# Two Fourier-attention layers on image planes: a kernel whose planes are normalized, mixed and squared in place, against one that keeps everything linear in modes and in one Gram matrix

## Chip, core and metric

The kernel runs on one core of one Trainium2 chip. The core has a matrix engine (TensorE, in the profile PE, with its weight loads as PEld), a vector engine (VectorE, DVE), a scalar engine (ScalarE, ACT), a general engine (GpSimd, POOL) and queues that start DMA transfers (SP, and the ACT queue). The metric is the device time of one execution in microseconds (us): 1426.25 us before the change, the median of three runs (1425.6 to 1430.25). A profiled execution is a run of its own; its span goes from its first instruction to its last.

## The reference

The input x holds 2 batches of 56 images of 128 x 128, all float32. Two layers of the same form follow each other; each adds its result to x. A layer first takes a group norm over the batch's images (32 groups of 4 neighbouring columns), and then:

```
xn   = inorm(xa)                          # each image: mean 0, variance 1
k, q, v = Spec(xn) + skip(xn)             # 1 -> 8 heads
attn = softmax(<q, k> / 128)              # 56 x 56 per head and batch
out  = Spec(attn v) + skip(attn v)        # 8 heads -> 1
att  = inorm(out + xa);  an = inorm(att)
h    = gelu(inorm(Spec(an)) + skip(an))   # M0
h    = inorm(Spec(h)) + skip(h)           # M1
y    = inorm(h) + att
```

`Spec` is a spectral convolution: the two-dimensional real Fourier transform, 32 x 16 of its modes multiplied by weights, and the transform back. `skip` multiplies by a number per head.

## The kernel before

Two sets of planes stay on chip, `X` (the running x) and `A` (work), each with h on the 128 partitions and (image, w) along them: 112 images of 128 columns. The modes of all images are tiles `spec` of 128 partitions (32 j + 16 c + kx, with c the real or imaginary part) by 8 t by 112 images. `layer` runs for each of the two layers, and does in this order:

- Group norm, per batch: sums over h by a matrix of ones (L340), subtraction (L350), squares (L352) and their sums (L353), scaling (L364), statistics of every image (L326), instance norm (L376, L378).
- Planes to modes: `to_rows` (L270, 112 matmuls of 64 columns with an image as weights), `to_modes` (L282, on four column tiles of 32; L289 exchanges real and imaginary part).
- `U xh` for eight heads (L386 to L388) while TensorE takes the Gram matrices (L394, 128 matmuls per batch, operands read at one w of all images). Scores (L406), softmax, the attention transposed.
- `D`, the output's modes: transposes (L446), products (L453) and sums over heads (L454, L455).
- The mix of images, in place, four w at a time: transposes (L462), copy (L464), matmuls (L467), copy back.
- `from_modes` three times (output, M0, M1): the modes go out to memory and come back turned (L300, L303), POOL reorders them (L308), matmuls on two column tiles (L312), a copy (L316), and matmuls of 512 columns (L319) into a use of its own: L474, L542 with gelu (L545), L557. Between them `to_rows` and `to_modes` again for M0 and M1, their norms (L508 to L528) and the residual (L538).
- The end: instance norm of h and the sum into `X` (L578 to L582); the second layer stores it.

`prepare` (L163) multiplies the weights of a layer out on POOL. A planner puts the instructions of each engine into an order by readiness and by their place in the source; buffers come from pools (`pm` four PSUM banks, `t2` four tiles, `spec` six). Every call of a float32 matmul becomes two weight loads and two matmul instructions; a transpose becomes one of each.

## Time and profile before

| what | value |
|---|---|
| median of three runs | 1426.25 us |
| span of the profiled execution | 1412.7 us |
| clock granted to TensorE, mean over the span | 0.747 |
| HBM read, written | 11.93 MB, 10.09 MB |
| DVE busy | 819.8 us |
| ACT busy | 306.0 us |
| POOL busy | 211.9 us |

The profile gives for each engine the time in which it ran an instruction. The clock line (PEclk) gives the speed that TensorE was granted, in tenths of full speed; 0.50 in a window is half speed. A row of the groups reads: line, engine, operation, output tile and input tiles, their shapes (partitions x elements), count, then busy time, mean time of one in ns, and the idle time of the engine ahead of it with what ended it. A row of the timeline reads: start, length, engine, line, operation, count. Matmul records overlap, so the length of a run divided by its count is the time from one to the next.

### The profile page before, as it was taken

What the parts mean: (1) busy time and instruction counts of PE and PEld (TensorE: products, weight loads), DVE (VectorE), ACT (ScalarE), POOL (GpSimd) and SP (SyncE); (2) the same over time, 40 slices, a digit from 0 to 9 for tenths busy, and PEclk for the clock granted to TensorE, in tenths of its full rate; (3) what the DMA queues carried; (4) which work ended last, traced back from release to release, by engine and by line L of the source; (5) the groups of instructions that cost most, each with busy time, mean ns of one, the idle gap of its engine ahead of it and who ended that gap; (6) DMA issues with size and microseconds to landing.
All of it is one profiled execution on the core that took longest, in us unless ns stands there. A gap on an engine that the chain in (4) does not pass through costs nothing.

```text
span 1412.7 us, 13545 instructions
## 1 busy us (share of the span) xinstructions
PE 1003.7 (71%) x4992; PEld 695.5 (49%) x4992; DVE 819.8 (58%) x2052; ACT 306.0 (22%) x536; POOL 211.9 (15%) x259
## 2 busy tenths in 40 slices
PE   5374899798778936948633849989877887287550
PEld 1151788346664823724212438944566556146320
DVE  2367452791116797528978581739411397873498
ACT  0222200002221203410352321010122112152024
POOL 6603040000001013011131110400000001301102
PEclk9777599665558977979866957986555599599685
DMA  9000000001000010010000000000100000100106
GB/s 260 0 1 1 0 1 1 1 0 26 0 1 1 1 27 0 1 27 1 1 0 1 0 0 1 1 0 0 26 0 1 0 1 0 27 1 1 26 16 193
DMA packets 38872, 22.89 MB, mean 16 GB/s; under 512 B 8606, under 2 KB 37654, under 8 KB 38806
## 3 DMA queue, kind: packets, MB, share of 16 engines
q1 hardware_dynamic: 37216, 20.19, 5.8%
q10 hardware_dynamic: 1590, 1.83, 0.5%
q8 instruction: 39, 0.64, 0.2%
q14 instruction: 27, 0.22, 0.1%
HBM read 11.93 MB, written 10.09 MB: 16 GB/s over the span
## 4 chain that ended last, share of the span: by engine, by line
PE 60%; DVE 22%; ACT 8%; issue 3%; DMA 3%; POOL 3%; SPq 1%; ACTq 0%; POOLq 0%; DVEq 0%
PE mm L270 12%; PE acc L394 9%; PE mm L467 9%; PE mm L319 9%; DVE rows L326 6%; PE mm L453 5%; PE acc L353 3%; PE mm L312 3%; ACT t L464 3%; DVE A L364 2%; DVE A L580 2%; DVE A L557 2%; PE mm L462 2%; PE acc L340 2%; ACT A L128 2%
## 5 line engine op out<-in xcount | busy, mean ns | idle before, releaser
L319 PE MATMUL mm<-c_gw,t 128*128 128x512 f32 x336 | 168.8, 646 | 31.1 <-ACT t L316 31.1
L270 PEld LDWEIGHTS mm<-c_fh,A 128*128 128x128 f32 x1344 | 168.7, 206 | 8.5 <-issue 3.9
L270 PE MATMUL mm<-c_fh,A 128*128 128x64 f32 x1344 | 172.8, 291 | 0.0
L467 PE MATMUL mm<-mixT,t 112*128 112x112 f32 x512 | 131.2, 438 | 46.5 <-ACT t L464 46.5
L467 PEld LDWEIGHTS mm<-mixT,t 112*128 112x128 f32 x512 | 114.1, 328 | 72.8 <-ACT t L464 72.8
L308 POOL COPY lc<-spec 64x128 f32<-64x128 f32 x84 | 52.7, 655 | 627.7 <-PE mm L312 339.0
L126 DVE COPY A<-mm 128x448 f32<-128x448 f32 x32 | 29.1, 908 | 188.2 <-PE mm L467 188.2
L326 DVE BATCH_NORM_STATS2 rows<-A 128x6 f32<-128x128 f32 x672 | 137.0, 275 | 0.1
L394 PE MATMUL acc<-A 128*56 128x56 f32 x1024 | 134.0, 312 | 0.0
L394 PEld LDWEIGHTS acc<-A 128*56 128x56 f32 x1024 | 128.6, 226 | 6.1 <-issue 3.2
L319 PEld LDWEIGHTS mm<-c_gw,t 128*128 128x128 f32 x336 | 65.2, 205 | 108.1 <-issue 52.9
L126 DVE COPY big<-mm 128x512 f32<-128x512 f32 (+1 forms) x50 | 48.2, 971 | 98.6 <-PE mm L270 98.2
L312 PE MATMUL mm<-c_gh,lc 64*64 64x128 f32 x672 | 51.1, 297 | 75.0 <-POOL lc L308 75.0
L128 ACT COPY big<-mm 128x512 f32<-128x512 f32 (+1 forms) x50 | 47.8, 956 | 204.5 <-PE mm L270 138.9
L312 PEld LDWEIGHTS mm<-c_gh,lc 64*64 64x64 f32 x672 | 40.0, 145 | 104.0 <-POOL lc L308 76.1
L353 PE MATMUL acc<-t,ones_gn 128*128 128x512 f32 x112 | 57.1, 665 | 47.6 <-ACT t L352 47.6
L453 PE MATMUL mm<-attnT,big 56*128 56x448 f32 x128 | 82.8, 822 | 3.7 <-DVE spec L454 3.6
L542 DVE SCALAR_TENSOR_TENSOR A<-A,s,mm 128x128 f32<-128x128 f32 x224 | 59.4, 341 | 28.3 <-PE mm L319 28.3
L316 ACT COPY t<-mm 128x512 f32<-128x512 f32 x42 | 24.6, 586 | 220.6 <-PE mm L312 220.6
L462 PE MATMUL mm<-c_ident,A 128*112 128x128 f32 x256 | 68.0, 421 | 0.0
L340 PE MATMUL acc<-X,ones_gn 128*128 128x512 f32 x112 | 60.4, 688 | 10.1 <-DMA X<-x 7.6
L464 ACT COPY t<-mm 112x512 f32<-112x512 f32 x64 | 37.5, 586 | 136.5 <-PE mm L462 136.5
(170 smaller groups left out, 1239.9 us busy)
## 6 DMA issues: line engine op xcount, KB each, us to landing
X<-x SPq DMA_DIRECT2D x14, 512.0 KB, 7.3
out<-X SPq DMA_DIRECT2D x28, 256.0 KB, 2.3
turned<-spec SPq DMA_DIRECT2D x48, 56.0 KB, 2.0
spec<-turned SPq DMA_DIRECT2D x12, 224.0 KB, 3.7
raw<-weights ACTq DMA_DIRECT2D x2, 544.0 KB, 5.0
c_gw<-const_gw ACTq DMA_DIRECT2D x1, 256.0 KB, 5.3
sm<-small ACTq DMA_DIRECT2D x2, 63.0 KB, 5.5
c_swap<-const_swap ACTq DMA_DIRECT2D x1, 64.0 KB, 5.7
```

Of the source, the lines that this page charges most:

```text
L126: nc.vector.tensor_copy(to, of)
L270: nc.tensor.matmul(py[:, 64 * e : 64 * e + 64], lhsT=A[:, i + e, :], rhs=fh, start=True, stop=True)
L312: nc.tensor.matmul(pz[64 * c : 64 * c + 64, N * e : N * e + N], lhsT=four, rhs=gh[:, c, :], start=True, stop=True,)
L319: nc.tensor.matmul(po, lhsT=z[:, N * e : N * e + N], rhs=gw, start=True, stop=True)
L326: nc.vector.bn_stats(rows[:, k, :], A[:, i, :])
L340: nc.tensor.matmul(acc, lhsT=ones_gn, rhs=X[:, i : i + 4, :], start=(i == lo), stop=(i + 4 == hi))
L353: nc.tensor.matmul(acc2, lhsT=ones_gn, rhs=sq, start=(i == lo), stop=(i + 4 == hi))
L394: nc.tensor.matmul(acc[:K, :K], lhsT=plane, rhs=plane, start=(w == 0), stop=(w == N - 1))
L453: nc.tensor.matmul(pv, lhsT=XT[:, b, n, t, :], rhs=aT[b], start=True, stop=True)
L462: nc.tensor.transpose(pt[:I, N * e : N * e + N], A[:, :, w + e], ident)
L464: nc.scalar.copy(xt[:I, :], pt[:I, :])
L467: nc.tensor.matmul(po[:, I * e : I * e + I], lhsT=xt[:I, N * e : N * e + N], rhs=mix, start=True, stop=True)
```

## The change

The whole of `fno_layers` and the constants are new; the weights' packing and the launch stay.

- **Layouts.** x lies as `X2`, images on 112 partitions (and two rows more, for the group norm's shift), with h and w along them. A second set `P` (`plane`) has w on the partitions, then h, then images. x is loaded in 16 pieces; `turned` transposes 8 rows of h at a time on TensorE, copies them into `plane` on ScalarE, and takes statistics on VectorE.
- **Norms.** The group norm is a factor and a shift per w and batch; it is applied to `plane` in eight chunks inside the first forward transform (`norm`), and to `X2` by `scale_x`. The means and variances of all instance norms come from the Gram matrix of the planes (`gram`, 128 matmuls of 112 x 112) and from sums over modes (`sums`).
- **Transforms.** `forward` contracts w with 32 columns of weights on four column tiles, transposes blocks of 32 x 32 on VectorE, and contracts h; `inverse` goes back to h in the same way and leaves kx on groups of 32 partitions. Nothing goes through memory.
- **Modes.** The multiplication of modes by weights is a matmul with 64 x 64 matrices that POOL builds (`build`, `build_m`). Scores, value products (`VT`), `D`, and the multipliers of M0 and M1 (`multiply`) use them on 64-row tiles. Four PSUM pairs of two banks serve all of it.
- **Planes are met three times**: when they are transposed, in the gelu loop, and in the output loop, where the old x is fetched again from memory (`back`). Layer 0 stores its result in memory, and transposes it for layer 1 at once.
- The scaled planes, with the attention's mix in the weights `Bs`, are multiplied in those two loops in place of the old mix.

The core of the diff:

```diff
-    X = planes.tile([N, I, N], F32, name="X")
-    A = planes.tile([N, I, N], F32, name="A")
+    X2 = xp.tile([J, N, N], F32, name="X2")
+    P = pp.tile([N, N * I], F32, name="P")
...
+    def turned(hs, rows):
+        p = pair()
+        for k, h in enumerate(hs):
+            for e in range(4):
+                T.transpose(p[:, k, I * e : I * e + I], X2[:I, h + e, :], ident[:I, :I])
+        dst = bass_slice(hs[0], hs[1] - hs[0])
+        S.copy(dst, p[:, :, : 4 * I].rearrange("p k (h i) -> p k h i", i=I))
+        for b in range(B):
+            V.bn_stats(rows[b], dst[:, :, :, K * b : K * b + K])
...
+    def forward(xf, prep=None):
+        mid = mp.tile([N, 32, I], F32, name="mid")
+        for c in range(0, 8, 2):
+            p = pair()
+            for k in range(2):
+                i = 14 * (c + k)
+                if prep:
+                    prep(c + k)
+                for q in range(4):
+                    T.matmul(
+                        p[32 * q : 32 * q + 32, k, :448].rearrange("p (h i) -> p h i", h=32),
+                        lhsT=C["fw"], rhs=plane[:, 32 * q : 32 * q + 32, i : i + 14], start=True, stop=True,
+                        tile_position=(0, 32 * q),
+                    )
+            V.transpose(
+                mid[:, :, 14 * c : 14 * c + 28].rearrange("p m (k i) -> p k i m", k=2),
+                p[:, :, :448].rearrange("p k (h i) -> p k i h", h=32),
+            )
...
+        for h in range(N):
+            T.matmul(gram, lhsT=plane[:, h, :], rhs=plane[:, h, :], start=(h == 0), stop=False)
...
+        scale_x(0, 8)
...
+        for t in range(8):
+            p = pair()
+            for r in range(2):
+                for a4 in range(4):
+                    for e in range(2):
+                        k = e ^ r
+                        T.matmul(
+                            p[64 * e : 64 * e + 64, k, I * a4 : I * a4 + I],
+                            lhsT=WU[64 * e : 64 * e + 64, t, 4 * k + a4, :], rhs=xf[64 * e : 64 * e + 64, t, :],
+                            start=True, stop=True, tile_position=(64 * e, 64 * e), skip_group_check=True,
+                        )
+            u = UX[t % 3]
+            evict(u.rearrange("p (k a) i -> p k (a i)", k=2), p[:, :, :448])
+            for b in range(B):
+                score(b, xft[:, I * t + K * b : I * t + K * b + 64], u, start=(t == 0), stop=False)
...
+        for t in range(8):
+            for a in range(HEADS):
+                for e in range(2):
+                    T.matmul(
+                        p[64 * e : 64 * e + 64, t // 4, I * (t % 4) : I * (t % 4) + I],
+                        lhsT=VT[:I, t, e, 64 * a : 64 * a + 64], rhs=AT[:I, a, :], start=(a == 0), stop=(a == 7),
+                        tile_position=(0, 64 * e), skip_group_check=True,
+                    )
...
+        for g in range(8):
+            for m in range(2):
+                p = pair()
+                for k in range(2):
+                    q = 2 * m + k
+                    T.matmul(
+                        p[:, k, :448], lhsT=C["gw"][32 * q : 32 * q + 32, :],
+                        rhs=Z[32 * q : 32 * q + 32, 4 * g : 4 * g + 4, :].rearrange("p h i -> p (h i)"),
+                        start=True, stop=False, tile_position=(32 * q, 0), skip_group_check=True,
+                    )
+                for k in range(2):
+                    for e in range(4):
+                        T.matmul(
+                            p[:, k, I * e : I * e + I], lhsT=X2[:, 32 * (2 * m + k) + 4 * g + e, :], rhs=Bs,
+                            start=False, stop=True, skip_group_check=True,
+                        )
+                dst = bass_slice(64 * m + 4 * g, 32).rearrange("p k h i -> p k (h i)")
+                S.activation(dst, p[:, :, :448], AF.Gelu)
+                hs = rp.tile([N, 1792], F32, name="ring")[:, :896].rearrange("p (k m) -> p k m", k=2)
+                V.tensor_tensor(hs, dst, dst, ALU.mult)
+                for k in range(2):
+                    q = 2 * m + k
+                    T.matmul(
+                        E[32 * q : 32 * q + 32, 0, :448], lhsT=ones[:, :32], rhs=hs[:, k, :],
+                        start=(g == 0), stop=(g == 7), tile_position=(0, 32 * q), skip_group_check=True,
+                    )
...
+        for g in range(8):
+            for m in range(2):
+                hs = (64 * m + 4 * g, 64 * m + 32 + 4 * g)
+                dst = xo[:, 2 * m : 2 * m + 2, 4 * g : 4 * g + 4, :]
+                back = rp.tile([N, 1792], F32, name="ring")[:I, :1024]
+                bk = back.rearrange("p (k h w) -> p k h w", k=2, h=4)
+                src = raw.rearrange("p (q r) w -> p q r w", r=32)[:, 2 * m : 2 * m + 2, 4 * g : 4 * g + 4, :]
+                nc.sync.dma_start(out=bk, in_=src)
+                p = pair()
+                for k in range(2):
+                    h = hs[k]
+                    T.matmul(p[:I, k, :], lhsT=Bs, rhs=X2[:, h : h + 4, :].rearrange("p h w -> p (h w)"), start=True, stop=False, skip_group_check=True)
+                for e in range(4):
+                    for k in range(2):
+                        q = 2 * m + k
+                        T.matmul(
+                            p[:I, k, N * e : N * e + N], lhsT=Z[32 * q : 32 * q + 32, 4 * g + e, :],
+                            rhs=C["gw"][32 * q : 32 * q + 32, :], start=False, stop=False, tile_position=(32 * q, 0),
+                            skip_group_check=True,
+                        )
+                for k in range(2):
+                    for e in range(4):
+                        T.matmul(
+                            p[:I, k, N * e : N * e + N], lhsT=plane[:, hs[k] + e, :], rhs=ig, start=False, stop=True,
+                            skip_group_check=True,
+                        )
+                V.scalar_tensor_tensor(
+                    dst.rearrange("p k h w -> p k (h w)"), p[:I], r3, back.rearrange("p (k m) -> p k m", k=2),
+                    ALU.mult, ALU.add,
+                )
+                to = (store if L == 0 else ov).rearrange("p (q r) w -> p q r w", r=32)
+                nc.sync.dma_start(out=to[:, 2 * m : 2 * m + 2, 4 * g : 4 * g + 4, :], in_=dst)
+                if L == 0:
+                    turned(hs, [s[:, 2 * g + m, :] for s in stats])
```

## The prediction

> **What bounds the kernel now.** I read the page's head first, then the chain of work that ended last, then the table of windows for the granted clock, then the groups by shape for prices.

> ```profile
> span 1412.7 us, 13545 instructions
> PE 1003.7 (71%) x4992; PEld 695.5 (49%) x4992; DVE 819.8 (58%) x2052; ACT 306.0 (22%) x536; POOL 211.9 (15%) x259
> PEclk9777599665558977979866957986555599599685
> PE 60%; DVE 22%; ACT 8%; issue 3%; DMA 3%; POOL 3%; SPq 1%; ACTq 0%; POOLq 0%; DVEq 0%
> ```

> TensorE is busy 71% of the span and is 60% of the chain, so it is the bound. But look at the clock line: it was granted full speed in hardly a third of the slices. The time is therefore made of three parts: columns streamed, the clock they were streamed at, and 409 us (1412.7 - 1003.7) in which TensorE stood. The next fence (table of windows; columns: stretch, length, busy time and records of PE, PEld, DVE, ACT, POOL, then clock, DMA share, GB/s) shows when the clock is granted.

> ```profile
> 148.00:172.00 24.00, 24.00 (x117) 21.47 (x117) 11.65 (x42) 9.74 (x22) 0.00 (x0) 0.50 0.00 1
> 178.00:190.00 12.00, 12.00 (x106) 10.25 (x109) 1.66 (x2) 2.03 (x2) 0.00 (x0) 1.00 0.01 1
> 194.00:238.00 44.00, 44.00 (x358) 44.00 (x357) 25.83 (x16) 0.20 (x1) 18.94 (x8) 1.00 0.01 1
> 265.50:289.70 24.20, 24.20 (x34) 10.50 (x34) 19.96 (x22) 0.58 (x1) 0.00 (x0) 0.50 0.00 1
> 294.00:298.00 4.00, 4.00 (x12) 1.86 (x10) 3.29 (x5) 0.00 (x0) 0.00 (x0) 1.00 0.00 0
> 316.00:430.00 114.00, 91.27 (x385) 78.33 (x385) 15.95 (x17) 32.65 (x47) 1.52 (x4) 0.50 0.04 9
> 440.00:470.00 30.00, 26.30 (x128) 12.82 (x129) 28.86 (x105) 2.93 (x5) 2.19 (x6) 1.00 0.00 1
> ```

> Being busy is not enough: 265.5 to 289.7 is 100% busy at 0.50. That is L453 (row below), which contracts over 56 of 128 partitions. 316 to 430 (the mix of images, 80% busy) also stays at 0.50; the dense 440 to 470 gets 1.00, and once granted it survives thinner work (194 to 238).

> **Prices.** The timeline gives runs of one instruction (start, length, engine, line, count); every float32 matmul is two such instructions (L319: 168 calls in the code, x336 on the page), a transpose is one.

> ```profile
> 580.82 25.07 PE L270 MATMUL mm<-c_fh,A 128*128 128x64 f32 x223
> 549.92 3.70 PE L319 MATMUL mm<-c_gw,t 128*128 128x512 f32 x8 [0.74 <-ACT t L316]
> 552.60 1.02 PE L319 MATMUL mm<-c_gw,t 128*128 128x512 f32 x2
> 553.55 1.09 PE L312 MATMUL mm<-c_gh,lc 64*64 64x128 f32 x16
> 555.38 3.70 PE L319 MATMUL mm<-c_gw,t 128*128 128x512 f32 x8 [0.74 <-ACT t L316]
> 265.47 24.26 PE L453 MATMUL mm<-attnT,big 56*128 56x448 f32 x32
> 317.66 2.05 PE L467 MATMUL mm<-mixT,t 112*128 112x112 f32 x8 [0.67 <-ACT t L464]
> 289.66 3.64 PE L446 MATMUL mm<-c_ident,spec 128*56 128x128 f32 x16
> 189.49 1.73 PE L282 MATMUL two<-big,c_fw 128*32 128x448 f32 x16
> 192.86 47.52 PE L394 MATMUL acc<-A 128*56 128x56 f32 x382
> ```

> At clock 1.00, L319 takes 433 ns for 512 columns: 0.85 ns a column. L270 has 64 columns (54 ns) but takes 112, so there the 128 weight columns set the pace (0.87 each). L467 takes 256 at clock 0.50 for 112 columns and 128 weights, so 128 at 1.00. L446: 228 at 0.50, so about 0.89 us for eight transposes at 1.00. L282 runs four column tiles: 108 ns each instead of 380, so they run side by side. L312 on two column tiles: 68 instead of 109. L394 takes 124 for only 56 columns; its operands are read with a stride of one image, which the new Gram matrix doesn't have.

> ```profile
> L126 DVE COPY big<-mm 128x512 f32<-128x512 f32 x42 | 42.8, 1027 | 98.6 <-PE mm L270 98.2
> L126 DVE COPY spec<-mm 128x448 f32<-128x448 f32 x6 | 3.7, 622 | 5.6 <-PE mm L289 5.6
> L557 DVE SCALAR_TENSOR_TENSOR A<-A,sm,mm 128x512 f32<-128x512 f32 x56 | 39.3, 735 | 31.4 <-PE mm L319 31.4
> L582 DVE TENSOR_TENSOR X<-X,A 128x512 f32<-128x512 f32 x38 | 25.7, 680 | 0.1
> L545 ACT ACTIVATE A<-A 128x512 f32<-128x512 f32 x56 | 33.9, 628 | 27.8 <-DVE A L542 27.8
> L245 ACT ACT_TABLE_LOAD x5 | 6.4, 1283 | 0.1
> L350 POOL TENSOR_TENSOR A<-X,gmw 128x512 f32<-128x512 f32 x16 | 23.5, 1498 | 91.7 <-DVE gmw L345 91.7
> X<-x SPq DMA_DIRECT2D x14, 512.0 KB, 7.3
> raw<-weights ACTq DMA_DIRECT2D x2, 544.0 KB, 5.0
> 5.00:34.00 29.00, 18.66 (x32) 7.04 (x32) 6.46 (x14) 2.52 (x3) 19.31 (x63) 0.89 1.10 290
> 11.20 0.16 DVE L499 TENSOR_TENSOR mb<-sm 128x1 f32<-128x1 f32 x1 [11.20 <-DMA sm<-small]
> ```

> VectorE and ScalarE cost about 1.04 and 0.9 ns an element plus some 150 to 200; a strided write (first row) 1.75 instead of 1.04. The input stage moves 290 GB/s (window 5 to 34). The last row matters too: L499 stands deep in the layer and runs at 11 us, so instructions are put in an order by readiness, not by the source.

> **The change, part by part.** It replaces everything, so I sum the new kernel, not a difference. Gone are the group norm on the planes, the separate mean and variance passes, the mix (L462 to L468, the 114 us from 316), the M0 and M1 residuals, and the turn through memory.

> *Load and transposes, once.* x (7.3 MB), the weights (1.1) and the constants (0.85 by the code) are 9.3 MB, at 290 GB/s 32 us; 128 transposes follow it, eight (0.9 us, twice that at half clock) per 1.6 us of load. With start and tail 38. The weights' POOL chain, some 20 us a layer by the 19.31 of POOL in that window, lies beside it; layer 1's runs on under layer 0.

> *Per layer:*
> - Norm factors: some 14 small operations at 0.2 to 0.4 us and a table load: 6.
> - Norm and forward transform: five VectorE passes over 1792 elements at 2.0 are 10; four 32x32 block transposes of 896 elements. No row shows that operation; between the contiguous rate (1.1) and the strided one (1.7) I take 1.7, because its writes step by 112 elements. TensorE (4 x 1.73) hides under these 17; the second transform adds 5. Sum 22. The norm pass might run at half of 2.0, so 17 is the low end.
> - Gram matrix: 256 instructions, between 97 (columns) and 128 ns (L467 halved); I take 117: 30, with hand-over 31. Scaling the planes (16 operations of 1024 elements, 1.2 to 1.6 us on VectorE) and building the mode matrices (8 POOL operations, about 2.9 us by twice L350) lie beside it. Without that cover: 13 us a layer and 10 us in layer 0.
> - Scores: per t, 32 instructions on diagonal 64x64 tiles at 60 ns (L312 scaled) and four of 448 columns, two side by side: 2.7 us; eight: 22, with hand-over 23.
> - Attention to the end of the first inverse transform: value products and their evictions 10 (softmax's 6.5 beside them), attention transposed 3, 256 instructions for D at 60 ns plus copy 16, adding and the M0 multiplier 5, sums 2, the scalar chain 5, factors as rows 1.3, spectrum 4.2, inverse 9, hand-overs 1.5: 57.
> - Gelu loop, 16 rounds: four instructions of 448 columns on 32-row tiles in pairs 0.76, sixteen of 112 columns and 128 weights 2.05, four for the squares' sum in column tiles 0.76: 3.57; ScalarE (0.95) and VectorE (1.1) are below it. 57.
> - Forward transform of h 15, multiplier and squares 4, sums 3, scalar chain with two table loads 6.5, rows 1.5, spectrum 5, inverse 9: 44.
> - Output loop, 16 rounds: four of 512 columns 1.73; sixteen of 128 columns on 32-row tiles 1.09; sixteen of 128 columns 2.0: 4.8, so 77. In layer 0 eight transposes more: 5.7, so 91. VectorE's 1.24 plus 1.1 for statistics stays below. So does the DMA: 0.92 MB read and written back is 3.2 us at 290 GB/s. New waits: the store of a round waits for VectorE, and behind it on SP stands the next round's fetch, which has two rounds of time (two ring buffers). The transposes wait for VectorE's sum of their own round; by readiness the next round's matmuls go ahead of them. In source order TensorE would stand 1.6 us (1.24 and a hand-over) sixteen times, 26.

> Layer 0: 6 + 22 + 31 + 23 + 57 + 57 + 44 + 91 + 2 for the last statistics = 333. Layer 1: 317. With 38 ahead and 4 for the last store: 692. Loops don't run at their TensorE sum: the old one repeats every 5.46 us (549.92 to 555.38) for 3.70 + 1.09 of matmuls, 14% over. On the four loops (282 us) that is 39. **Span 731.** Before, the median of 1426.25 stands 13.5 us over the span of the profiled execution, so the forecast is **745 us**.

> **Two places where rows are thin.** Row tiles: the trace has only column tiles. Side by side they cost what I put; one after another they cost 12 a loop, 10 in the scores, 7 in the value products, 9 in the rest: 50 a layer, 100 in all. [...] In the rows of before, L312 on its tiles starts at 553.55, before L319's 552.60 + 1.02 is over, with no gap to be seen, so I price a switch between nothing and 0.1 us: about 200 switches, at most 20.

> Clock: the gelu loop begins after a stretch with TensorE mostly idle. At 0.50 a round takes 7.1 us, and the share of rows times streaming time in it is (1.5 x 0.5 + 4.1 x 0.65 + 1.5 x 1) / 7.1, or 0.69. L467's stretch has 0.62 by the same count (1.5 us on 112 rows and 0.9 of transposes in rounds of 3.6) and stays cold; 172 to 178 us, L394 alone, has 0.75 and ends warm:

> ```profile
> 172.00:178.00 6.00, 6.00 (x46) 5.88 (x47) 1.01 (x1) 0.00 (x0) 0.00 (x0) 0.51 0.00 0
> ```

> So it can go either way. [...]

> **Rivals.**
> - *The gelu loop stays at half clock.* 16 x (7.1 - 3.57) = 57 a layer, 114 in all: 860. For it: the 0.69 above and the stretch from 316. Against: the squares' part is full-height. Chance 0.25.
> - *Row tiles run one after another:* 845. For it: nothing shows them; against: column tiles do run side by side. Chance 0.15. Both rivals together: 960, chance 0.08.
> - *Leaner than the sum:* norm passes at 1.0, transposes at 1.1, no 14%: about 670. Chance 0.09.
> - *Slower than before:* TensorE keeps being held up for short times, so that the clock is never granted anywhere, and tiles run one after another. Then Gram is 61, scores 75, value products, D and rest 123, gelu 162, the h part 60, output 183 (212 in layer 0), norm and transform 30: about 700 and 731 a layer with the 6 for the factors, 1,490 in all. [...] Chance 0.03.

> **The numbers.** Forecast 745, chance 0.40. The range is 670 to 960: it takes in the lean case, both single rivals and their sum. A measurement of this kernel can tell about 0.3% from no change. Faster by more than that 0.96, within it 0.01, slower 0.03.

> **What would show it.** Right: a gelu loop of about 65 us a layer at clock 1.00, the Gram matrix's 256 instructions in about 30 us, an output loop of 85 to 105, and 0.8 us for a pair of 32-row tiles. Wrong: clock 0.50 in the gelu loop; row tiles whose starts are a full 380 ns apart; a block transpose of well over 1.7 us; a load stage beyond 45 us; TensorE waiting in a loop on the DMA that fetches the old x back.

## The result, and the profile after

The changed kernel took **787.01 us** (median of four runs, 777.49 to 796.58) against 1425.92 us (median of four runs of the kernel before on the same chip): a ratio of 0.5499, 95% interval 0.5461 to 0.5537. The forecast was 745 us, with a range of 670 to 960. The direction and the size of the gain came out; 42 us of it did not. The profiled execution is one of these runs, of 777.49 us with a span of 775.7; the others have spans of 783.4 to 794.8 at lower mean clocks (0.872 to 0.859 against 0.890), and the slowest, 2.5% above the fastest, counts as a slow run and is left out of the ratio.

The head of the page and the shares of the chain, as shown of before:

```profile
span 775.7 us, 10768 instructions
PE 617.2 (80%) x4866; PEld 435.4 (56%) x4866; DVE 290.6 (37%) x392; ACT 122.8 (16%) x142; POOL 78.4 (10%) x140
PEclk9955689999659999699999989999955999969999
PE 61%; DVE 22%; ACT 6%; DMA 4%; POOL 4%; issue 2%; ACTq 0%; DVEq 0%
```

TensorE is the bound as before (61% of the chain), but its stand-still went from 409 to 158.5 us (775.7 - 617.2), and the clock line now has full speed in most slices. Where the rest lies is seen in the table of windows (columns as in the prediction: PE, PEld, DVE, ACT, POOL, clock, DMA share, GB/s):

```profile
5.00:36.50 31.50, 20.92 (x129) 16.95 (x129) 17.30 (x31) 13.67 (x16) 19.83 (x68) 1.00 0.94 251
36.50:88.50 52.00, 23.35 (x103) 21.87 (x103) 13.11 (x40) 5.11 (x10) 33.24 (x50) 0.51 0.03 11
106.60:132.00 25.40, 25.40 (x259) 25.29 (x259) 18.73 (x17) 0.27 (x1) 0.84 (x1) 1.00 0.04 6
217.00:235.00 18.00, 15.48 (x56) 9.60 (x58) 2.42 (x3) 1.83 (x2) 0.00 (x0) 0.55 0.00 1
235.00:294.00 59.00, 54.64 (x326) 32.07 (x322) 14.20 (x13) 11.92 (x13) 0.00 (x0) 0.99 0.00 1
332.00:449.00 117.00, 91.30 (x708) 65.40 (x704) 41.39 (x50) 14.48 (x16) 3.33 (x2) 1.00 0.41 122
697.50:772.00 74.50, 72.91 (x564) 51.40 (x560) 20.54 (x16) 0.00 (x0) 0.00 (x0) 1.00 0.61 180
```

The second row is the largest surprise: 52 us behind the load in which TensorE works 23 us at half clock. The fourth is the gelu loop's start at 0.55; the rest of the loop has 0.99. Against the last row (layer 1's output loop, 73 of 74.5 us busy), layer 0's output loop above it stands 26 of 117 us. Stage by stage, with borders at the first starts of L350, L468 and L483, at the end of the last score product (L504), and at the first starts of L662, the second L350 and L751 (the forecast's 14% is put into the loops):

| stage | forecast | layer 0 | layer 1 |
|---|---|---|---|
| load, transposes, norm factors up to the first transform (layer 1: factors) | 44 (6) | 88.6 | 3.3 |
| norm and forward transform | 22 | 18.0 | 15.2 |
| Gram matrix with hand-over | 31 | 26.7 | 26.7 |
| scores | 23 | 27.0 | 27.0 |
| attention to the first inverse transform | 57 | 57.0 | 54.7 |
| gelu loop | 65 | 76.9 | 78.1 |
| h part | 44 | 38.1 | 38.1 |
| output loop with end | 106 (92) | 118.7 | 81.6 |

The columns add up to 732 for the forecast and 775.7 measured. Three stages are too long: the front by 45, the two gelu loops by 25, layer 0's output loop by 13. The others together give back about 39.

**The front.** TensorE's timeline behind the load (start, length, engine, line, tiles, shapes, count, and in brackets the idle time ahead with what ended it), and the one row of VectorE's that matters:

```profile
36.21 0.27 PE L279 MATMUL pair<-C,mixed 128*128 128x128 f32 x1
39.30 3.57 PE L290 MATMUL pair<-C,ring 128*128 128x16 f32 x16 [2.82 <-DVE ring L284]
...
68.08 0.48 PE L279 MATMUL pair<-C,mixed 128*128 128x128 f32 x1 [14.35 <-POOL mixed L256]
...
84.83 0.59 PE L427 MATMUL pair<-pk,C 128*128 128x4 f32 x2
88.59 3.96 PE L350 MATMUL pair<-P,C 128*32 128x448 f32 x20 [3.17 <-DVE P L443]
```

```profile
40.33 0.16 DVE L424 TENSOR_TENSOR pk<-pk,mv 128x2 f32<-128x2 f32 x1
```

The statistics are complete at 40.5 us, about when the forecast has them. The matmul that reads them (L427) starts at 84.83. Between stand the transposes and matmuls of `prepare` (L279, L290) for both layers: they are ahead of it in TensorE's queue, and the fourth transpose waits 14.35 us for POOL, which first builds layer 0's mode matrices. Nothing of layer 1's preparation is needed there.

**A round of the gelu loop**, at clock 1.00:

```profile
281.02 1.02 PE L662 MATMUL pair<-mid,C 32*128 32x448 f32 x4
281.97 0.92 PE L669 MATMUL pair<-Bs,X 114*128 114x112 f32 x6
283.23 0.94 PE L679 MATMUL pair<-ring,ones 128*32 128x448 f32 x4 [0.33 <-DVE ring L676]
284.10 1.37 PE L669 MATMUL pair<-Bs,X 114*128 114x112 f32 x10
285.40 1.02 PE L662 MATMUL pair<-mid,C 32*128 32x448 f32 x4
```

It repeats every 4.38 us (281.02 to 285.40). The squares' matmuls (L679) stand in the queue behind six of the next round's sixteen, and wait 0.33 us there for VectorE's squares.

**A round of layer 0's output loop:**

```profile
353.55 0.96 PE L326 MATMUL pair<-C,X 112*128 112x112 f32 x8 [1.47 <-DVE X L766]
354.35 1.88 PE L751 MATMUL pair<-X,Bs 114*112 114x512 f32 x4
356.16 1.13 PE L755 MATMUL pair<-C,mid 32*112 32x128 f32 x16
357.22 2.00 PE L762 MATMUL pair<-gvr,P 128*112 128x128 f32 x16
360.69 0.96 PE L326 MATMUL pair<-C,X 112*128 112x112 f32 x8 [1.47 <-DVE X L766]
```

It repeats every 7.14 us, and TensorE stands in it for the sum (L766) of its own round before each group of transposes. Nothing of the next round has been put ahead of them.

### The profile page after: what moved, and what is told of

Read it like the earlier page. It is cut to its first block, busy times and chain, and to the rows that moved or that the text cites. A ratio compares the mean times of both kernels' runs of the same rounds, so it can differ in the third digit from the quotient of the medians.

```text
span 775.7 us, 10768 instructions
## 1 busy us (share of the span) xinstructions
PE 617.2 (80%) x4866; PEld 435.4 (56%) x4866; DVE 290.6 (37%) x392; ACT 122.8 (16%) x142; POOL 78.4 (10%) x140
## 4 chain that ended last, share of the span: by engine, by line
PE 61%; DVE 22%; ACT 6%; DMA 4%; POOL 4%; issue 2%; ACTq 0%; DVEq 0%
PE pair L762 8%; PE pair L669 7%; PE pair L751 7%; PE pair L468 6%; PE pair L755 4%; PE pair L679 4%; DVE ring L676 4%; ACT P L674 3%; DVE mid L355 3%; PE pair L581 3%; DMA X<-x 3%; DVE mid L384 3%; DVE X L766 3%; PE pair L616 3%; PE pair L515 2%; PE pair L504 2%
## 5 line engine op out<-in xcount | busy, mean ns | idle before, releaser
L669 PEld LDWEIGHTS pair<-Bs,X 114*128 114x128 f32 x512 | 68.9, 210 | 46.0 <-issue 46.0
L669 PE MATMUL pair<-Bs,X 114*128 114x112 f32 x512 | 80.1, 306 | 0.0
L766 DVE SCALAR_TENSOR_TENSOR X<-pair,sd,ring 112x1024 f32<-112x1024 f32 x32 | 41.1, 1284 | 97.0 <-PE pair L762 97.0
L762 PE MATMUL pair<-gvr,P 128*112 128x128 f32 x512 | 64.0, 278 | 0.0
L751 PE MATMUL pair<-X,Bs 114*112 114x512 f32 x128 | 60.4, 594 | 0.0
L762 PEld LDWEIGHTS pair<-gvr,P 128*112 128x112 f32 x512 | 57.6, 177 | 4.2
L330 DVE BATCH_NORM_STATS2 stats<-P 128x6 f32<-128x448 f32 x64 | 36.8, 618 | 42.8 <-ACT P L328 42.7
L468 PE MATMUL pair<-P 128*112 128x112 f32 x512 | 50.7, 262 | 0.0
L468 PEld LDWEIGHTS pair<-P 128*112 128x112 f32 x512 | 50.5, 178 | 0.0
L679 PE MATMUL pair<-ring,ones 128*32 128x448 f32 x128 | 33.3, 601 | 13.2 <-DVE ring L676 13.2
L662 PE MATMUL pair<-mid,C 32*128 32x448 f32 x128 | 36.9, 655 | 4.7 <-DVE mid L384 4.7
L350 PE MATMUL pair<-P,C 128*32 128x448 f32 x256 | 34.2, 604 | 7.7 <-DVE P L443 7.7
L462 DVE TENSOR_TENSOR X<-X,gvr 112x1024 f32<-112x1024 f32 x32 | 36.5, 1217 | 0.1
L319 DVE COPY P<-pair 128x896 f32<-128x896 f32 (+1 forms) x16 | 18.3, 1155 | 37.4 <-PE pair L515 37.2
## 6 DMA issues: line engine op xcount, KB each, us to landing
ring<-weights ACTq DMA_DIRECT2D x2, 544.0 KB, 8.2
```

The lines of the kernel that those rows point to most:

```text
L468: T.matmul(gram, lhsT=plane[:, h, :], rhs=plane[:, h, :], start=(h == 0), stop=False)
L662: T.matmul(p[:, k, :448], lhsT=C["gw"][32 * q : 32 * q + 32, :], rhs=Z[32 * q : 32 * q + 32, 4 * g : 4 * g + 4, :].rearrange("p h i -> p ( ...
L669: T.matmul(p[:, k, I * e : I * e + I], lhsT=X2[:, 32 * (2 * m + k) + 4 * g + e, :], rhs=Bs, start=False, stop=True, skip_group_check=True,)
L679: T.matmul(E[32 * q : 32 * q + 32, 0, :448], lhsT=ones[:, :32], rhs=hs[:, k, :], start=(g == 0), stop=(g == 7), tile_position=(0, 32 * q), ...
L751: T.matmul(p[:I, k, :], lhsT=Bs, rhs=X2[:, h : h + 4, :].rearrange("p h w -> p (h w)"), start=True, stop=False, skip_group_check=True)
L762: T.matmul(p[:I, k, N * e : N * e + N], lhsT=plane[:, hs[k] + e, :], rhs=ig, start=False, stop=True, skip_group_check=True,)
```

## The experiments

Three theories answer to the three stages: the front's loss is the **place in TensorE's queue**; the output loop's is the wait of transposes for their own round; the gelu loop's is the squares' wait and the **clock at its start**. Their rivals are in the expectations.

**1. Layer 1's preparation later:** `behind` calls `prepare(1)`, and stands behind layer 0's Gram matrix.

```diff
         rl, rk, rc = rr[:, :K], rr[:, K : K + 1], rr[:I, K + 1 : K + 2]
+        if behind:
+            behind()
```

> Layer 1's preparation is moved in the source behind layer 0's Gram matrix; nothing else changes. Theory A (its matmuls and copies stand in the queues of TensorE, VectorE and ScalarE ahead of layer 0's first norm, and wait for POOL's second chain): the first transform starts near 50 us instead of 88.6, the span falls by 35 to 45 us, to about 735. Theory B (layer 0 is held by the load, or by POOL's matrices): the first transform moves by under 10 us. If the second preparation then stands in front of the scores, 5 to 10 us come back there.

Measured: 777.96 us (ratio 0.5455, 0.5421 to 0.5489). The first transform starts at 64.06 instead of 88.59 and the Gram matrix at 80.98 instead of 106.64, but the scores only at 124.89 instead of 133.67. TensorE's timeline ahead of the scores:

```profile
121.42 3.54 PE L290 MATMUL pair<-C,ring 32*128 32x4 f32 x16 [1.59 <-DVE ring L284]
124.89 1.39 PE L517 MATMUL pair<-modes,WU 64*64 64x112 f32 x12
```

Layer 1's transposes and matmuls, begun at 107.9, end in front of the next stage now (L517 is its first product with the mode matrices). The place in the queue is the cause of these 25 us of the front, but behind the Gram matrix it costs most of them again: 9 are left at the scores, where theory A had put the whole gain at 35 to 45.

**2. Layer 0's transposes one round late.**

```diff
                 if L == 0:
-                    turned(hs, [s[:, 2 * g + m, :] for s in stats])
+                    if late:
+                        turned(*late.pop())
+                    late.append((hs, [s[:, 2 * g + m, :] for s in stats]))
```

> In layer 0's output loop the transposes of a round are issued after the matmuls of the next round. Theory A (TensorE stands still for VectorE's sum before the transposes, 1.5 us of each 7.13): rounds of 5.6 to 5.8, the loop of 114 us falls by 20 to 24, the span to about 753. Theory B (the fetch of the old x and the store set the round): 7.1 stays, no change.

Measured: 757.24 us (ratio 0.5312, 0.5278 to 0.5347).

```profile
341.88 0.93 PE L326 MATMUL pair<-C,X 112*128 112x112 f32 x8
...
347.36 0.93 PE L326 MATMUL pair<-C,X 112*128 112x112 f32 x8
```

The round is 5.48 us, with no wait in it: 1.66 less than 7.14, and the whole loop is 26 us shorter (92.7 instead of 118.7). The wait was all that it lost.

**3. The squares' matmuls one round late.**

```diff
-                for k in range(2):
-                    q = 2 * m + k
-                    T.matmul(
-                        E[32 * q : 32 * q + 32, 0, :448], lhsT=ones[:, :32], rhs=hs[:, k, :],
-                        start=(g == 0), stop=(g == 7), tile_position=(0, 32 * q), skip_group_check=True,
-                    )
+                if last:
+                    squares(*last.pop())
+                last.append((g, m, hs))
+        squares(*last.pop())
```

> In the gelu loop the two matmuls that sum the squares of a round are issued after the matmuls of the next round. Theory A (TensorE waits 0.33 us per round for VectorE's product): rounds of 4.05 instead of 4.38, 5 us a layer, 10 in all. Theory B (the round is TensorE's own work, weight loads included): 4.3 or more, less than 3 us in all.

Measured: 760.12 us (ratio 0.533, 0.5296 to 0.5363), span 759.6. In this kernel L672 is the 32-row product, L679 that with `Bs`, and L662 the squares:

```profile
276.94 0.95 PE L662 MATMUL pair<-ring,ones 128*32 128x448 f32 x4
277.82 1.02 PE L672 MATMUL pair<-mid,C 32*128 32x448 f32 x4
278.77 2.04 PE L679 MATMUL pair<-Bs,X 114*128 114x112 f32 x16
280.74 0.95 PE L662 MATMUL pair<-ring,ones 128*32 128x448 f32 x4
```

A round is 3.80 us (276.94 to 280.74), just the three parts laid end to end: the wait and the refilling behind it had cost 0.58. Layer 1's loop is 67.7 us instead of 78.1; layer 0's only falls to 72.4, because it stays at 0.50 longer (from about 213 to 240 us). The two loops give 15 us, as much as the profiled spans differ by (775.7 and 759.6); the rest of the 27 between the medians is of the size of the spread between executions.

**4. Three dummy matmuls ahead of the first inverse transform,** to have the clock up.

```diff
+        for _ in range(3):
+            T.matmul(E[:I, 0, :], lhsT=Bs, rhs=X2[:, 0:4, :].rearrange("p h w -> p (h w)"), start=True, stop=True, skip_group_check=True)
         spectrum(rows[:, 0, :], D, rows[:, 1, :], y0)
```

> Three matmuls of 114 rows and 512 columns, whose result is not used, are issued while VectorE forms the spectrum ahead of the first inverse transform. Theory A (the gelu loop starts at half clock because TensorE was idle ahead of it): the clock is 1.00 from the loop's start, 5 us a layer are saved, 10 in all. Theory B (the share of rows and streaming time in the loop itself is too thin to open the clock, as in the stretch of 114 us before): the clock falls back to 0.50 within the loop, no change or worse. The matmuls may delay the inverse transform by 1 to 3 us a layer.

Measured: 783.25 us (ratio 0.5499, 0.5463 to 0.5535). The clock does rise ahead of the inverse transform (0.89 from 209 to 216 us), and is gone when the loop begins. The window over the loop's start:

```profile
216.00:250.00 34.00, 33.83 (x106) 19.15 (x106) 4.48 (x5) 3.67 (x4) 0.00 (x0) 0.50 0.00 0
```

TensorE is busy 33.83 of 34 us at half clock. Theory B has the fall, but not what follows: the same loop, with the same rows, runs at 1.00 afterwards.

**5. The changed kernel again,** as base for the next three.

> The changed kernel once more, without an edit, as the base of the three that follow on the same chip. A theory that its 777 to 797 us are spread between executions expects a median of 778 to 792 here, and the first forward matmul at 85 to 92 us again.

Measured: 784.19 us (776.7 to 791.32; ratio 0.5543, 0.5512 to 0.5573). The 777 to 797 are spread between executions.

**6. The preparation woven in.** Layer 0's six groups stand between the Gram matrix's instructions, layer 1's between rounds of the gelu loop.

```diff
         for h in range(N):
+            if h % 20 == 4 and steps:
+                steps.pop(0)()
             T.matmul(gram, lhsT=plane[:, h, :], rhs=plane[:, h, :], start=(h == 0), stop=False)
...
             for m in range(2):
+                if later and g > 0 and m == 0:
+                    later.pop(0)()
```

> The weights' preparation stays on POOL ahead, but its TensorE part leaves the front: layer 0's three transposes and 24 matmuls are woven between the Gram matrix's instructions, layer 1's whole preparation is issued after layer 0's softmax operands and its TensorE part stands between rounds of the gelu loop. Theory queue order (the 45 us lost ahead of the first transform were TensorE's queue alone): the statistics' matmul at about 41 us and the first transform at about 45 to 49 instead of 88.6; Gram 31 to 34 us instead of 25 and the gelu loop of layer 0 about 8 longer, because those matmuls cost TensorE some 8 us a layer wherever they stand; in all 20 to 30 us less than the changed kernel, about 755 to 765 median. Theory POOL chain (the building of the mode matrices on POOL is the path): the scores wait for the matrices until about 110 us or later, and 10 us or less is gained.

Measured: 774.93 us (ratio 0.5457, 0.5441 to 0.5474); 9 us of the 20 to 30. The front is as forecast:

```profile
40.97 0.56 PE L440 MATMUL pair<-pk,C 128*128 128x4 f32 x2 [3.60 <-DVE pk L437]
45.65 7.77 PE L362 MATMUL pair<-P,C 128*32 128x448 f32 x56 [4.12 <-DVE P L456]
```

The statistics' matmul starts at 40.97 and the first transform at 45.65. So the queue's place is shown to be the cause of the 45 us. Much is given back at two places. The Gram stage takes 44 us instead of 27. In the groups of that stretch, `scale_x` (L475 here) and POOL's building of matrices are both slow; the third row is `scale_x` in the changed kernel, where it ran without POOL:

```profile
L475 DVE TENSOR_TENSOR X<-X,gvr 112x1024 f32<-112x1024 f32 x16 | 32.8, 2111 | 0.1
L312 POOL TENSOR_TENSOR WT<-tc,C 128x1024 f32<-128x1024 f32 x4 | 11.6, 2922 | 0.0
```

```profile
L462 DVE TENSOR_TENSOR X<-X,gvr 112x1024 f32<-112x1024 f32 x32 | 36.5, 1217 | 0.1
```

VectorE needs 2111 ns for what it did in 1217, POOL 2922 for what took it 1956. VectorE's late operands then hold up the last group of the preparation by 7.34 us. The second place is layer 0's gelu loop: 98 us instead of 77, with a mean clock of 0.75 from 186.5 to 287 us.

**7. TensorE's idle time filled ahead of the inverse transform:** ten matmuls, six behind the sums and four behind the factors' rows.

```diff
+        idle(6)
         k3 = sm.tile([I, 3], F32, name="k3", bufs=1)
...
+        idle(4)
         Bs = sm.tile([N, J], F32, name="Bs", bufs=1)[:J, :I]
```

> Ten matmuls of 512 columns over 114 rows whose result nobody reads fill TensorE's idle time in the scalar chain ahead of the first inverse transform (six behind the sums, four behind the factors' rows), so that TensorE isn't idle from about 195 us on. Theory clock kept (a clock once granted is lost only by idling): the clock stays at 1.00 from before 195 us through the gelu loop, whose length falls from 77 to about 71 us a layer; less 2 us of delay in the chain, 6 to 10 us gained in all. Theory load step (the clock falls at the start of the dense loop whatever came before, as in the run with three such matmuls, where 34 us went at 0.50): the loop still has 17 us or more at 0.50, 77 us or more, and the kernel is 0 to 15 us slower than the changed one.

Measured: 794.24 us (ratio 0.5601, 0.5584 to 0.5617), 10 slower than the changed kernel on the same chip.

```profile
210.00:214.00 4.00, 3.50 (x32) 2.90 (x32) 2.79 (x3) 1.28 (x1) 0.00 (x0) 1.00 0.00 0
214.00:217.50 3.50, 0.07 (x2) 0.00 (x0) 3.49 (x3) 0.00 (x0) 0.00 (x0) 0.97 0.02 5
217.50:235.00 17.50, 17.45 (x52) 9.36 (x52) 2.18 (x2) 1.83 (x2) 0.00 (x0) 0.50 0.00 0
```

The inverse transform has full clock. Then TensorE stands for 3.5 us while VectorE finishes its block transposes (3.49 busy), and the loop that follows has 0.50; in layer 1 the same pause is followed by 34 us at 0.50. That the clock is "lost only by idling" fits, but not with the idle time that the expectation meant: the middle row points at the pause right ahead of the loop.

**8. That pause filled too:** four matmuls that read the second and third quarter of the planes as soon as these are transposed.

```diff
         Z = inverse(s1)
+        for q in (1, 1, 2, 2):
+            T.matmul(
+                E[:, 0, :448].rearrange("p (h i) -> p h i", h=16), lhsT=ones, rhs=Z[:, 0:16, 28 * q : 28 * q + 28],
+                start=True, stop=True, skip_group_check=True,
+            )
```

> The filled chain, and beyond it four matmuls that read the second and third quarter of the inverse transform's planes (two each), so that the 3.5 us in which TensorE stood between the inverse transform and the gelu loop is filled as well. Theory idle gap (the clock falls at the loop's start because TensorE stood just ahead of it): the clock stays at 1.00 into the loop, whose length is 70 to 72 us a layer. Theory thin mix (the loop's own mix is too thin for the clock to be granted soon, whatever stands ahead of it): 17 us or more at 0.50 again, 77 to 90 us a layer.

Measured: 778.79 us (two runs; ratio 0.5476, 0.5447 to 0.5504).

```profile
214.90:222.40 7.50, 6.73 (x40) 4.23 (x40) 6.23 (x4) 1.22 (x1) 0.00 (x0) 1.00 0.01 2
222.40:235.00 12.60, 12.60 (x74) 7.51 (x74) 2.24 (x3) 2.75 (x3) 0.00 (x0) 1.00 0.00 0
```

The loop starts at 222.44 with 1.00 and keeps it, in layer 1 as well (from 587 to 655 us 1.00): 68.4 us in each layer instead of 76.9 and 78.1. The kernel differs from the seventh run by these four matmuls alone, so here the pause is shown to be what loses the clock. With all fourteen dummies the stretch from the scores to the loop is 6 to 7 us a layer longer than in the changed kernel, which eats most of the gain.

**9. The gelu loop without its 32-row matmuls.**

```diff
-                for k in range(2):
-                    q = 2 * m + k
-                    T.matmul(
-                        p[:, k, :448], lhsT=C["gw"][32 * q : 32 * q + 32, :],
-                        rhs=Z[32 * q : 32 * q + 32, 4 * g : 4 * g + 4, :].rearrange("p h i -> p (h i)"),
...
```

> The gelu loop without its four matmuls on 32-row tiles (the part of the planes that comes out of the inverse transform is left out of the gelu's argument), so TensorE is left with full-height and 114-row operands, and the loop need not wait for the inverse transform either. A round at 1.00 is 4.38 less 1.0, about 3.4 us, 54 in all. Theory thin mix (32 rows are what holds the clock back): at most 7 us at 0.50, 54 to 58 us a layer. Theory load step (any dense loop behind the idle chain is held at 0.50 first): 17 us or more at 0.50, 62 to 68 us a layer.

Measured: 711.98 us (two runs; ratio 0.5006, 0.498 to 0.5032).

```profile
215.50:225.00 9.50, 7.28 (x60) 6.32 (x58) 4.74 (x4) 2.36 (x3) 0.00 (x0) 1.00 0.01 2
550.00:553.50 3.50, 3.50 (x22) 3.50 (x22) 1.01 (x1) 0.92 (x1) 0.00 (x0) 0.63 0.00 0
```

Layer 0's loop has 1.00 from its first round, layer 1's loses the clock for some 3.5 us and has it back; the loops are 46 and 47.5 us. The load step theory falls. The loop no longer waits for the inverse transform either, so the pause ahead of it is gone with the rows; but TensorE now stands inside the first round, for 2.23 us in layer 0 and 2.22 in layer 1, until the squares are there. Layer 0 keeps its clock over that pause, layer 1 loses it 1.7 us behind it. So this run does not tell the rows from the pause. Layer 1's quick return is one instance, and run 12 has returns as quick with the 32-row matmuls in place.

**10. Runs 2, 3 and 6 together.**

> Three edits together: the preparation woven in, layer 0's transposes one round late, the squares' matmuls one round late. If the terms add: 20 to 30 from the front, 24 to 27 from layer 0's output loop, 10 to 17 from the two gelu loops, so 54 to 74 less than the changed kernel on this chip: about 710 to 730 median. If the gelu loop's time at half clock grows as it becomes denser, the last term is lost: 725 to 745.

Measured: 714.84 us (708.69 to 719.44; ratio 0.5023, 0.4992 to 0.5054): 69 below the changed kernel on the same chip, where the three alone had given 9 (run 6), 26 (the loop of run 2) and 15 (the two loops of run 3). The rest comes from layer 0's gelu loop, which had cost run 6 most of its gain: 77 us here, 98 there. In that loop the clock is at 0.50 for 24 us here and for 50 there; these runs don't tell how much of this the edits caused and how much is chance.

**11. The same with the preparation at other places:** operands multiplied out on POOL, layer 0's matmuls in the norm stage, layer 1's in the scalar chain.

```diff
+        if L == 0 and c == 3:
+            first(2)
+            second(1)
...
-                    V.tensor_tensor(
+                    G.tensor_tensor(
```

> As the run of three edits together, but the preparation's factors are multiplied out on POOL from a copy that ScalarE makes, and its matmuls stand where TensorE waits: layer 0's between the statistics and the end of the first forward transform, layer 1's in the scalar chain ahead of the gelu loop instead of inside it. If queue position is all: the Gram matrix back at 25 us (was 43 with the preparation between its instructions), layer 0's gelu loop back at about 72 from 79; the norm stage up to 5 us longer, the chain up to 3; in all 10 to 25 us less than the run of the three together, 690 to 705 median. If POOL's work beside VectorE slows both: the norm stage 10 us longer or the scores wait, and nothing is gained, 705 to 720.

Measured: 719.17 us (709.34 to 727.26; ratio 0.5005, 0.4972 to 0.5038), no difference from run 10 that can be told. The Gram stage is back at 27 us and layer 0's gelu loop at 71, but the norm stage takes 29 instead of 17, and the stretch from the sums to the first inverse transform 24.4 instead of 13. One row of VectorE and one of POOL, from a run of 723.94 us, show why for the norm stage:

```profile
58.19 12.31 DVE L462 TENSOR_SCALAR P<-P,gv,sh 128x1792 f32<-128x1792 f32 x1
```

```profile
60.27 7.64 POOL L310 TENSOR_TENSOR WT<-tc,C 128x1024 f32<-128x1024 f32 x4
```

A single norm pass lasts 12.31 us, from 58.19 to 70.50, where the changed kernel's took 1.18 on average (row in the next section). POOL runs without a gap from 57.57 to 69.52 beside it. The other stretch has the same on a smaller scale: two VectorE operations of 0.33 us each in the changed kernel (L409) take 5.75 from 180.38 on, beside 5.74 of POOL's building from 180.32 on.

**12. Run 10 with the pause filled:** run 4's three matmuls ahead of the inverse transform and run 8's four behind it.

> The run of three edits together, with three dummy matmuls ahead of the inverse transform (as in the fourth run) and the four that read the second and third quarter of its planes behind it, so that TensorE no longer stands for 3.5 us just ahead of the gelu loop. Theory idle gap: both loops start at 1.00 and keep it; layer 1's is 60 to 63 us (16 rounds of 3.79) instead of 72, layer 0's 67 to 72 instead of 80; 15 to 20 us less, 695 to 702 median. If three matmuls are too few ahead of the inverse transform for the clock to be up by then, the loops start at 0.50 and stay there for 17 us or more: 712 to 722.

Measured: **699.32 us** (median of six, 696.64 to 707.06; ratio 0.4927, 0.4902 to 0.4953), the fastest of all.

```profile
520.00:583.50 63.50, 63.50 (x407) 38.14 (x409) 17.82 (x17) 14.67 (x16) 0.00 (x0) 1.00 0.00 1
225.50:228.70 3.20, 3.20 (x13) 1.67 (x11) 0.41 (x1) 0.92 (x1) 3.20 (x3) 0.50 0.00 0
242.50:249.20 6.70, 6.70 (x26) 3.77 (x23) 0.66 (x1) 1.00 (x2) 0.00 (x0) 0.50 0.00 0
```

Layer 1's loop is 60.7 us, at 1.00 throughout (69.2 in run 10). Layer 0's, with the preparation inside, is 71.6 and still loses the clock twice, as the last two rows show, with TensorE busy throughout and no pause ahead. Both times matmuls of the preparation, of 16 or 4 columns, end less than 2 us before.

## Why the prediction came out as it did

**The failed step** is in the load: "The weights' POOL chain, some 20 us a layer by the 19.31 of POOL in that window, lies beside it; layer 1's runs on under layer 0." POOL's part did lie beside the load. But I had priced the preparation by POOL alone. Its TensorE part, three transposes and 24 matmuls a layer, stood nowhere in the sum, and what stood behind it in TensorE's queue waited with it: the matmul whose operands were complete at 40.5 us started at 84.83. The first transform is 45 us later than forecast by that, as much as the whole span is over the forecast; run 6 has the first transform at 45.65, where the forecast has 44. That the total missed by no more than that is in part luck: three stages were 83 us too long, and the others gave back 39.

**Output loop of layer 0, wrong branch.** I wrote both: "by readiness the next round's matmuls go ahead of them. In source order TensorE would stand 1.6 us (1.24 and a hand-over) sixteen times, 26." The order is that of the source, and run 2 measures 1.66 us a round and 26 in all. The 14% already put 13 there, so 13 are over. In layer 1 the same loop runs with no hand-over at all (73 of 74.5 us busy), and there the 14% was too much.

**Gelu loop, three small terms.** 57 plus 8 was forecast, 76.9 measured. The parts end to end, at full clock, are 60.7 (run 12, layer 1) instead of 57: the two 32-row products of a round have 0.95 us against 0.76, the product with `Bs` 1.97 against 2.05. The squares' wait, which I had not seen as a step of its own, makes 68.4 of it (run 8). The start at half clock costs the rest, 8.5. The 14% was to cover such things, and was half of what they came to.

**The clock rival** (the whole loop at 0.50, 860 us) came true only for the loop's first 17 to 20 us. No trace of before shows which clock this loop's mix gets, so its price at 1.00 was an estimate; measured, layer 0's loop has 0.55 from 217 to 235 us and 0.99 from there to 294. What I argued from, the share of rows in use, is not by itself what takes the clock away: run 8 keeps 1.00 with the same rows (222.4 to 290 us). In run 7 it goes behind a pause of 3.5 us (0.97 in the pause, 0.50 in the 17.5 us behind it). In run 4 being busy didn't bring it back for 34 us: TensorE is busy for 33.83 of them, at 0.50.

The pause is not the whole story. In layer 0 of the changed kernel TensorE stands only 1.81 us ahead of the loop, and the clock goes 1.5 us into the loop (217.29 to 218.75). It goes without any pause right ahead of it, too, while TensorE is busy with the sums' matmuls of one column (L616):

```profile
195.40:198.20 2.80, 2.80 (x31) 2.80 (x30) 0.00 (x0) 2.23 (x2) 0.00 (x0) 1.00 0.01 3
198.40:201.40 3.00, 3.00 (x17) 3.00 (x18) 0.17 (x1) 0.00 (x0) 0.00 (x0) 0.50 0.00 0
```

In run 12, too, it goes with TensorE busy, less than 2 us behind matmuls of 16 or 4 columns, and that behind two of three such groups. That a few microseconds of very short instructions count like a pause is a guess that no run tests. What the return waits for stays open. In the two layers it took 17 and 20 us in the changed kernel, 27 and 17 in run 3, 38 and 20 in run 4, 20 and 34 in run 7, and 3.4 in layer 1 of run 9; but also 3.4 and 6.8 in layer 0 of run 12, with all the rows of the changed kernel, so the mix of rows does not decide it alone.

In the traces of before and of the changed kernel, apart from their ends, every stretch at one clock lasts a whole multiple of 3.41 us. Two times three neighbouring stretches of the changed kernel, each window just inside its stretch:

```profile
198.30:215.30 17.00, 10.88 (x55) 9.32 (x54) 9.83 (x19) 1.49 (x2) 0.00 (x0) 0.50 0.00 0
215.40:218.70 3.30, 1.49 (x10) 0.76 (x9) 1.84 (x2) 0.00 (x0) 0.00 (x0) 1.00 0.00 0
218.80:235.75 16.95, 14.72 (x52) 8.75 (x50) 2.19 (x2) 1.83 (x2) 0.00 (x0) 0.50 0.00 1
560.15:573.70 13.55, 7.43 (x37) 6.42 (x39) 7.51 (x17) 1.49 (x2) 0.00 (x0) 0.50 0.00 0
573.80:577.10 3.30, 1.18 (x14) 0.83 (x10) 3.30 (x3) 0.00 (x0) 0.00 (x0) 1.00 0.00 0
577.20:597.60 20.40, 17.50 (x58) 10.24 (x58) 2.80 (x3) 1.83 (x2) 0.00 (x0) 0.50 0.00 1
```

From change to change these are 17.07, 3.41, 17.07, 13.65, 3.41 and 20.48 us. Whether it matters where a pause falls between two changes, no run tests.

**Row tiles** run side by side: four instructions of 448 columns in 0.95 us (281.02 to 281.97) where one after another would be 1.52 at the prediction's 0.85 ns. The serial rival falls. No trace of before shows row tiles, so the 0.76 us put for these four was carried over from column tiles; 0.95 stands in its place, and the sixteen of 128 columns, put at 1.09, take 1.06 (356.16 to 357.22). A switch between tilings can cost little: run 3's round, with three of them, has 3.80 us against 3.57 by prices without any, so by these prices one costs 0.08 us at most, an estimate.

**Right as sized:** the load itself (the last transposes end at 36, though at 251 GB/s instead of 290), attention to the first inverse transform (57.0 and 54.7 against 57), and the block transpose, taken between bounds:

```profile
L355 DVE STREAM_TRANSPOSE mid<-pair 128x896 f32<-128x896 f32 x16 | 26.0, 1696 | 2.6 <-PE pair L350 2.3
L443 DVE TENSOR_SCALAR P<-P,gv,sh 128x1792 f32<-128x1792 f32 x10 | 11.5, 1180 | 0.0
```

The transpose takes 1.70 us, as put. The norm pass is near the low end that was named (1.18, where half of 2.0 is 1.0). Too dear were the Gram matrix (25.4 us for its 256 instructions, 99 ns each, instead of 117) and the h part (38 instead of 44); too cheap the scores (27 instead of 23).

**The 13.5 us between span and median** were taken for a constant. A run's time stands 1.8 us over its own span (777.49 and 775.7); the other 9.5 between it and the median of 787.01 are the spread of executions. The term was right in size for the wrong reason.

## What to carry to other kernels

When a step is said to lie beside other work, list what it issues on every engine and find what stands behind each of those instructions in its queue: here matmuls that waited for POOL held up what stood behind them, the first transform starting at 88.59 us instead of the 45.65 of run 6. In a loop whose round ends with another engine's result, have the first engine use that result one round later; it was 26 us here for a few lines of code. Ahead of a loop that needs full clock, look for the last pause of TensorE: four matmuls that depend on the work just ahead of the loop kept 1.00 (run 8) where ten earlier ones alone left 0.50 (run 7). Look for matmuls of few columns there as well: on or just behind them the clock went from 1.00 to 0.50 without a pause (198.3 us in the changed kernel, twice in run 12).
